# Where the second expert's list is written and where the registers are loaded, in a fused attention and mixture-of-experts block

## The chip, the cores and the metric

The kernel runs on one core of a Trainium2 chip. The metric is the device time of one execution in microseconds. Before the change three runs took 1684.58, 1686.65 and 1686.75 us, so the median is 1686.65 us. The execution that the hardware profiler recorded took 1661.85 us, and the span from its first to its last instruction is 1660.0 us.

## The reference

One transformer block on x of shape (2, 2048, 256), float32. A conditioning vector gives shifts, scales and gates (`sa, ca, ga, sb, cb, gb`); the gates are kept at least 0.25 away from zero.

```python
h = _layernorm(x, axis=-1) * (1 + ca) + sa
x = x + ga * _L0_attn_ref(h, ...)        # 2 query heads of 128, one key and value head, rope, causal
h = _layernorm(x, axis=-1) * (1 + cb) + sb
x = x + gb * _L0_ffn_ref(h, ...)
```

The second part is a mixture of eight experts with a threshold of its own for each token:

```python
gate = jax.nn.softmax(x @ Wg + bg, axis=-1)
thr = jax.nn.sigmoid(x @ Wt + bt) * MAX_THRESHOLD
adapted = gate - thr
mask = (adapted >= 0).astype(x.dtype)
w = adapted * mask          # then divided by its sum over the experts
h = jax.nn.gelu(jnp.einsum('td,edf->etf', x, W1) + b1[:, None, :])
eo = jnp.einsum('etf,efd->etd', h, W2) + b2[:, None, :]
out = jnp.einsum('te,etd->td', w, eo)
```

With the inputs used, 2640, 2609, 2370, 2710, 2418, 2886, 3614 and 1806 of the 4096 tokens have a weight above zero for experts 0 to 7. The kernel computes an expert only for the tokens on its list.

## The kernel before

**Two phases.** `attention` works through 32 tiles of 128 tokens, the two batches in turn in groups of 4, 4, 4, 2, 1 and 1 tiles. `experts` then works through items of 256 tokens of one expert, expert after expert. Line numbers here are those of the kernel before, which the profile names too.

**Attention and its planner.** Every step of this phase (a few instructions on one engine) is handed to `Plan.add` with an engine, an assumed cost, what it follows, what it takes of a fixed number of buffers and gives back, a rank, and a time `late` after which its result is there. `Plan.run` then plays the steps through once, always giving an idle engine the ready step of the lowest rank, and emits the instructions in the order found. So one more step, or another cost or rank, can move every later step on all engines. A tile's steps are layer norm (statistics on VectorE, the power to -1/2 on GpSimd, L425 and L426), projections, rope, scores (L541), exponentials on ScalarE (L568), their transposes (L614), the product with the values (`pav`, L624), the output projection (`po`, L658), the residual, the second layer norm (`hx`), a copy of it as high and low halves (L690) which goes to the DRAM tensor `feats`, and the logits (`pl`). For each group `gate_steps` computes weights (`entry`), counts tokens on TensorE (`pc`, L797 and L800) and from that each token's place on the list of every expert (`place`, up to L818). An indirect DMA from GpSimd's queue for each tile then writes the entries of expert 0 to its list in DRAM (`scatter`, L821). Each of these waits for the one before it on the list.

**Work ahead.** When 24 tiles are listed, the head of list 0 is read (L919) and two items of expert 0 (AHEAD = 2, 512 tokens) are worked on within attention: `fetch` gathers their rows from `feats` (GpSimd, L897), transposes them by a DMA of SyncE's queue (L906) and joins the halves (VectorE, L912); then come matmuls `pha` (L963), Gelu (L971), matmuls `pya` (L980), and `result` (L987, L990). These steps have rank 1000, behind everything else. Their first matmuls and their Gelu follow the last tile's exponentials, which need another table on ScalarE. In the same way the whole list 0 is read (L1018) and the item after these two is fetched to xT (`_next`). `total` (L865 to L884) writes the count of every list to `counts`, less the 512 tokens worked on ahead (for expert 0, 2128 remain), and, for each list, two numbers that steer how the next one is written: how many items it has that are followed by another one (at most NP = 8), and 8 less that.

**The expert phase.** It opens with a barrier of all engines. Each engine has a program of its own with loops, and waits on semaphores. `count` (L1051) loads a number of `counts` into a register of an engine; TensorE and ScalarE load eight, VectorE nine, before their first work. An item is fetched in a chain: GpSimd copies two indices for each partition (`at`, L1312) and gathers the rows to `xr` (L1270, two indirect DMAs); SyncE transposes xr to `xp` (L1116); VectorE joins the halves into `xT` (`ready`, L1212) when TensorE has finished the item's first matmuls. There is one xr, one xp and one xT. TensorE runs eight pairs of matmul groups, `h` (L1158) and `y` (L1149), with Gelu on ScalarE between them (L1184). VectorE adds the bias (`yb`, L1236), names the rows (`who`, L1240), clears the second half of `yo` where an item has only 128 tokens (L1247) and multiplies with the gates (`yo`, L1248). GpSimd adds yo to the rows of the output by indirect DMAs (L1301). VectorE names rows and writes yo only when the scatter before the last has landed. ScalarE issues the weights of expert e + 2, 2 MB, when it reaches expert e (L1193, L1196).

**How lists 1 to 7 are written.** A list has 32 tiles of entries, in 8 parts of 4 tiles. GpSimd writes a part of list e + 1 (`write`: two copies, L1283 and L1286, and four scatters, L1291) within the fetch of an item of expert e, between that item's gathers and the scatter of a result. As many parts as are not carried so are written ahead of the expert's items. Ahead of everything, `write(1, 0, 0)` writes part 0 of list 1 once more, so that every later part has one before it to wait for. SyncE reads list e + 1 (L1106) when all its parts have landed, and GpSimd begins the items of expert e + 1 only after that.

## Time and profile before

| what | value |
| --- | --- |
| median of three runs | 1686.65 us |
| profiled execution | 1661.85 us |
| its span | 1660.0 us |
| TensorE busy | 1613.9 us, 97% of the span |
| VectorE, ScalarE busy | 659.0 us (40%), 584.4 us (35%) |
| GpSimd busy | 904.5 us (54%) |
| mean granted TensorE clock | 0.992 of full speed |
| last matmul ahead ends, first expert matmul starts | 482.2 us, 490.42 us |
| last matmul ends | 1647.5 us |

PE is TensorE's matmuls, PEld its weight loads, DVE VectorE, ACT ScalarE, POOL GpSimd and SP SyncE; a q behind a name is the engine's sequencer or its DMA queue. A row of the timeline has start and length in microseconds, engine, line, operation, output and inputs, the number of instructions, and in brackets how long the engine was idle before it and what ended that. The chain of waits is followed back from the last instruction: at each step to what released it. In the table by stretches, each engine's busy time in a stretch stands in the order PE, PEld, DVE, ACT, POOL, and behind it the granted clock as a share of full speed, the share of the 16 DMA engines, and GB/s.

### The profile page before, as it was taken

The page shows a single profiled execution, that of the slowest core. Times are in us where ns is not written, and L with a number is a line of the kernel's source. Part 1 is how long each engine was busy: PE and PEld are TensorE (multiplying, and loading weights), DVE is VectorE, ACT ScalarE, POOL GpSimd, SP SyncE. Part 2 cuts the span into 40 slices and gives each one's busy share as a digit, 9 for nine tenths or more (in the row PEclk, how much of TensorE's full clock was granted, in tenths as well). Part 3 has the DMA queues.
Part 4 walks back from the last instruction along what each step waited for, and adds up shares of the span by engine and source line. Part 5 has one row for each costly group of instructions (what it writes and reads, how often), then busy time and mean ns, then how long its engine had stood idle before and what let it go on. Part 6 is the DMA issues. An engine that isn't in the chain of part 4 may idle for free.

```text
span 1660.0 us, 26742 instructions
## 1 busy us (share of the span) xinstructions
PE 1613.9 (97%) x7666; PEld 1347.2 (81%) x7666; DVE 659.0 (40%) x2148; ACT 584.4 (35%) x1416; POOL 904.5 (54%) x1037
## 2 busy tenths in 40 slices
PE   8999999999989979999999999999999999999996
PEld 5667677777768868888888888888888888888886
DVE  7987656656532322223222222222322232222322
ACT  3555555555522222222222222222222222222222
POOL 5563522211237767756776774676677477644443
PEclk9999999999989999999999999999999999999999
DMA  5411000000133353335335333533533333333432
GB/s 182 150 39 34 26 30 29 14 14 13 33 84 60 60 106 57 60 62 111 57 64 112 59 59 66 102 61 62 112 60 59 59 58 60 66 57 57 66 57 46
DMA packets 166045, 106.36 MB, mean 64 GB/s; under 512 B 111136, under 2 KB 157344, under 8 KB 165856
## 3 DMA queue, kind: packets, MB, share of 16 engines
q0 software_dynamic: 42064, 46.84, 17.8%
q1 hardware_dynamic: 116048, 46.22, 11.8%
q10 hardware_dynamic: 7872, 12.58, 2.4%
q8 instruction: 26, 0.43, 0.1%
q14 instruction: 35, 0.29, 0.1%
HBM read 50.39 MB, written 31.87 MB: 50 GB/s over the span
## 4 chain that ended last, share of the span: by engine, by line
PE 61%; DMA 3%; POOL 3%; issue 3%; POOLq 1%; DVE 0%; DVEq 0%; SPq 0%
PE h L1158 31%; PE y L1149 31%; DMA xp<-xr 2%; POOL out L1301 2%; DMA xr<-feats,at 1%; POOL list L1291 1%; POOL xr L1270 0%; DMA out<-yo,who 0%; DMA sign_p_next<-g_sb_r_next 0%; DMA g_sb_r_next<-feats,next_at 0%; POOLq L1051 0%; POOL out L1333 0%; POOL at L1312 0%; POOLq L1099 0%; POOLq L1312 0%
## 5 line engine op out<-in xcount | busy, mean ns | idle before, releaser
L1158 PE MATMUL h<-xT,w 128*128 128x256 f32 (+1 forms) x2752 | 659.2, 372 | 19.9 <-DVE xT L1212 11.6
L1149 PE MATMUL y<-w,g 128*128 128x256 f32 x2640 | 654.1, 379 | 0.0
L1184 ACT ACTIVATE g<-h,b_sb 128x256 f32<-128x256 f32 (+1 forms) x688 | 320.5, 466 | 849.9 <-PE h L1158 848.3
L1158 PEld LDWEIGHTS h<-xT,w 128*128 128x128 f32 x2752 | 514.0, 191 | 90.1 <-DVE xT L1212 13.3
L1149 PEld LDWEIGHTS y<-w,g 128*128 128x128 f32 x2640 | 498.5, 190 | 66.1
L1301 POOL DMA_INDIRECT out<-yo,who x173 | 282.5, 1633 | 212.7 <-DVE yo L1248 161.2
L1212 DVE COPY xT<-xp 128x512 uint16<-128x512 uint16 x172 | 67.9, 437 | 628.2 <-PE h L1158 602.8
L1291 POOL DMA_INDIRECT list<-new,to x228 | 232.8, 1021 | 99.3 <-POOL new L1286 46.7
L1270 POOL DMA_INDIRECT xr<-feats,at x172 | 174.3, 1013 | 100.9 <-POOL at L1312 70.2
L541 PE MATMUL psc<-kT,qT 128*128 128x512 f32 (+3 forms) x320 | 143.7, 534 | 0.0
L624 PE MATMUL pav<-pT,v 128*128 128x256 f32 x544 | 142.9, 385 | 0.0
L552 DVE TENSOR_SCALAR_CACHE_REDUCE s<-psc 128x512 f32<-128x512 f32 (+3 forms) x160 | 96.0, 604 | 67.4 <-PE psc L541 48.9
L568 ACT ACTIVATE s<-s,nmx 128x512 f32<-128x512 f32 (+3 forms) x160 | 103.8, 650 | 47.0 <-DVE nmx L559 46.8
L624 PEld LDWEIGHTS pav<-pT,v 128*128 128x128 f32 x544 | 95.9, 190 | 28.8 <-issue 20.9
L1236 DVE TENSOR_TENSOR yb<-y,b_bc 128x256 f32<-128x256 f32 x165 | 62.7, 420 | 136.1 <-PE y L1149 136.1
L618 ACT COPY pT<-ptr 128x512 f32<-128x512 f32 (+1 forms) x144 | 76.8, 564 | 47.9 <-PE pav L624 32.5
L1227 DVE SCALAR_TENSOR_TENSOR gate<-gb_bc,mcur,part 128x256 f32<-128x256 f32 x172 | 75.8, 482 | 3.0
L425 POOL TENSOR_SCALAR rstdf<-mvf 128x1 f32<-128x1 f32 x32 | 8.2, 257 | 122.7 <-DVE mvf L421 70.7
L614 PE MATMUL ptr<-ident,s 128*128 128x128 f32 x544 | 72.6, 274 | 2.1 <-ACT s L568 1.9
L614 PEld LDWEIGHTS ptr<-ident,s 128*128 128x128 f32 x544 | 63.1, 141 | 13.1 <-ACT s L568 4.9
L1312 POOL COPY at<-sheet 128x2 int32 x85 | 62.9, 740 | 14.5 <-DMA xp<-xr 13.5
L821 POOL DMA_INDIRECT list<-entry,place x32 | 33.5, 1048 | 62.4 <-DVE place L818 26.8
(159 smaller groups left out, 1098.6 us busy)
## 6 DMA issues: line engine op xcount, KB each, us to landing
w<-in_w ACTq DMA_DIRECT2D x12, 1024.0 KB, 7.8
x<-in_x SPq DMA_DIRECT2D x32, 128.0 KB, 2.1
out<-x SPq DMA_DIRECT2D x32, 128.0 KB, 1.7
feats<-hp SPq DMA_DIRECT2D x32, 128.0 KB, 1.7
w<-in_w SPq DMA_DIRECT2D x4, 1024.0 KB, 9.1
list<-new,to POOLq DMA_INDIRECT x228
out<-yo,who POOLq DMA_INDIRECT x173, 3.9
xr<-feats,at POOLq DMA_INDIRECT x172
```

What stands on the lines that cost most here:

```text
L541: nc.tensor.matmul(ps[:, :w], st["qT"][:, h, :], kT[:, ds(c * SC, w)], start=True, stop=not last)
L552: nc.vector.tensor_scalar(s[:, :w], st["sc", h, c][:, :w], 1.0, None, ALU.mult, ALU.max, accum_out=st["mx", h][:, c : c + 1],)
L568: nc.scalar.activation(s[:, :w], s[:, :w], AF.Exp, bias=st["nmx", h], accum_out=st["den"][:, h, c : c + 1],)
L614: nc.tensor.transpose(ptr[:, j, h, :], s[:, ds((c0 + j) * P % SC, P)], ident)
L618: nc.scalar.copy(pT[:, :m], st["ptr", c0][:, :m])
L624: nc.tensor.matmul(st["pav"][:, : NH * P], v[:, c0 + j, :], st["pT", c0][:, j].rearrange("p h t -> p (h t)"), start=(c0 + j == 0), stop=(c ...
L1149: last = pe.matmul(ys[c], gs[f % 4][:, ts(c, P)], weights[e][1][:, f, :], start=(f == 0), stop=(f == NF - 1),)
L1158: last = pe.matmul(hs[f % 4][:, :w], weights[e][0][:, k, ts(f, P)], xT[:, k, :w], start=(k == 0), stop=(k == KD - 1),)
L1184: act.activation(gs[f % 4][:, :w], hs[f % 4][:, :w], AF.Gelu_apprx_tanh, bias=b1_sb[:, at : at + 1],).then_inc(sem["act"], 1)
L1270: pool.indirect_dma_start(out=xr[:, ts(c, 2 * D)], out_offset=None, in_=feats, in_offset=bass.IndirectOffsetOnAxis(ap=at[:, c : c + 1], ax ...
L1291: pool.indirect_dma_start(out=lists[e], out_offset=bass.IndirectOffsetOnAxis(ap=to[:, j : j + 1], axis=0), in_=new[:, j, :], in_offset=Non ...
L1301: pool.indirect_dma_start(out=rows, out_offset=bass.IndirectOffsetOnAxis(ap=who[:, c : c + 1], axis=0), in_=yo[:, c, :], in_offset=None, b ...
```

## The change

1. **Two parts of list 1 in attention.** The first FRONT = 2 parts of list 1, tiles 0 to 7 in the order of tokens (the first eight of batch 0), are scattered in attention, each tile by one indirect DMA from `entry` and `place`, as list 0 is, with a rank 10 higher. In the expert phase expert 0's items carry at most 6 parts (2 to 7), the numbers in `counts` are capped to suit, and `write(1, 0, 0)` becomes one scatter of tile 0.
2. **Items ahead.** Their first matmuls follow the last tile's last `pav` step (`last_sum`) in place of its exponentials; their Gelu still follows the exponentials. The read of the head of list 0 no longer follows the last scores.
3. **The next item first.** The fetch of the item behind those two has rank 999.
4. **Registers in the plan.** Steps `hold` at the end of the plan load the registers before the barrier: eight each on TensorE (behind its last matmul ahead) and ScalarE, nine on VectorE, four on GpSimd, two on SyncE. `count` then takes the register, and loads only what was not held.
5. **The last half item.** If the last item of expert 7 has 128 tokens, its rows and its result go to `who_end` and `yo_end`; VectorE neither waits for the scatter before nor clears a half.

```diff
+FRONT = 2
@@ attention, tile_steps and gate_steps
+        last_sum[:] = n_p[-1:]
-        def scatter(j):
+        def scatter(e, j):
             nc.gpsimd.indirect_dma_start(
-                out=lists[0],
-                out_offset=bass.IndirectOffsetOnAxis(ap=place[:, at + j, 0:1], axis=0),
-                in_=entry[:, at + j, 0, :],
+                out=lists[e],
+                out_offset=bass.IndirectOffsetOnAxis(ap=place[:, at + j, e : e + 1], axis=0),
+                in_=entry[:, at + j, e, :],
...
         for j in range(m):
-            listed.append(plan.add(
-                "POOL", 1.1, lambda j=j: scatter(j), after=[n] + listed[-1:], rank=r + 10.0,
-                late=1.5,
-            ))
+            for e in (0, 1):
+                if e == 0 or at + j < FRONT * NW:
+                    listed[e].append(plan.add(
+                        "POOL", 1.1, lambda e=e, j=j: scatter(e, j), after=[n] + listed[e][-1:],
+                        rank=r + 10.0 * (e + 1), late=1.5,
+                    ))
@@ total
+        nc.vector.tensor_scalar(n[:, :1], n[:, :1], float(NP - FRONT), None, ALU.min)
         nc.vector.tensor_copy(counts[:, E : 2 * E], n)
         nc.vector.tensor_scalar(
-            counts[:, 2 * E : 3 * E], n, -1.0, float(NP), ALU.mult, ALU.add
+            counts[:, 2 * E : 2 * E + 1], n[:, :1], -1.0, float(NP - FRONT), ALU.mult, ALU.add
+        )
+        nc.vector.tensor_scalar(
+            counts[:, 2 * E + 1 : 3 * E], n[:, 1:], -1.0, float(NP), ALU.mult, ALU.add
         )
@@ items ahead, the next item, registers
-    n_front = low("SP", 0.1, read_front, listed_ahead + last_score, late=2.5)
+    n_front = low("SP", 0.1, read_front, listed_ahead, late=2.5)
-                "PE", 1.74, lambda f0=f0, first=first: first(f0), [n_x, l_first[0]] + before_gelu,
+                "PE", 1.74, lambda f0=f0, first=first: first(f0),
+                [n_x, l_first[0]] + last_sum,
...
+    def next_(eng, cost, do, after=(), **how):
+        return plan.add(eng, cost, do, after=after, rank=999.0, **how)
+    n_behind = next_("DVE", 0.4, behind, [n_s, n_flag])
+    fetch(lambda c: next_at[:, c : c + 1], "_next", [n_behind], lambda: kept.xT, low=next_)
...
+    def hold(name, eng, columns):
+        def load():
+            kept.count[name] = {at: register(nc, eng, counts, at) for at in columns}
+        return load
+    low("PE", 2.0, hold("PE", nc.tensor, range(E)), [n_total] + n_ahead)
+    low("ACT", 2.0, hold("ACT", nc.scalar, range(E)), [n_total] + n_a)
+    low("DVE", 2.2, hold("DVE", nc.vector, [*range(E), skip]), [n_total, n_behind])
+    low("POOL", 1.0, hold("POOL", nc.gpsimd, [skip, 0, E, 2 * E]), [n_total])
+    low("SP", 0.5, hold("SP", nc.sync, [0, E]), [n_total, n_s])
@@ experts, SyncE's read of a list
-                    sync.wait_ge(sem["written"], (e * NP + 1) * (16 * NW))
+                    sync.wait_ge(sem["written"], (e * NP - FRONT) * (16 * NW) + 16)
@@ experts, VectorE's item
-                    dve.wait_ge(sem["added"], t * (16 * CI) + 2 * (16 * CI))
+                    end = e == E - 1 and parts < CI
+                    if not end:
+                        dve.wait_ge(sem["added"], t * (16 * CI) + 2 * (16 * CI))
                     dve.tensor_copy(
-                        who, mcur[:, :, 2:3].bitcast(I32).rearrange("p c o -> p (c o)")
+                        who_end if end else who,
+                        mcur[:, :, 2:3].bitcast(I32).rearrange("p c o -> p (c o)"),
                     ).then_inc(sem["named"], 1)
...
-                    if parts < CI:
+                    if parts < CI and not end:
                         dve.memset(yo[:, parts:, :], 0.0)
                     dve.tensor_tensor(
-                        yo[:, :parts], yb[:, :parts], gate[:, :parts], ALU.mult
+                        (yo_end if end else yo)[:, :parts], yb[:, :parts], gate[:, :parts],
+                        ALU.mult,
                     ).then_inc(sem["biased"], 1)
@@ experts, GpSimd
-                write(1, 0, 0)
+                pool.indirect_dma_start(
+                    out=lists[1],
+                    out_offset=bass.IndirectOffsetOnAxis(ap=place[:, 0, 1:2], axis=0),
+                    in_=entry[:, 0, 1, :],
+                    in_offset=None,
+                ).then_inc(sem["written"], 16)
...
                 with pool.If(single > 0):
-                    add(t0 + 1, 1)
+                    add(t0 + 1, yo_end, who_end, 1)
```

More of the change, by code (lines that the diff above doesn't have):

```diff
@@ L160, in adaln_block_kernel @@
         xT=const.tile([P, KD, TI], F32, name="xT"),
+        count={},
     )
@@ L186, in adaln_block_kernel @@
     at = ep.tile([P, CI], I32, name="at")
+    yo_end = ep.tile([P, 1, D], F32, name="yo_end")
+    who_end = ep.tile([P, CI], I32, name="who_end")
     mcur = ep.tile([P, CI, ENT], F32, name="mcur")
@@ L193, in adaln_block_kernel @@
         tc, nc, lists, feats, out.rearrange("b t d -> (b t) d"), counts, ident, b1_sb, b2_bc,
-        gb_bc, w1, w2, weights, xr, xp, kept, gs, gate, part, yb, sheets, at, mcur, to, new,
+        gb_bc, w1, w2, weights, xr, xp, kept, gs, gate, part, yb, yo_end, who_end, sheets, at, mcur, to, new,
         place, entry, hs, ys,
@@ L836, in gate_steps @@
         for j in range(m):
-            listed.append(plan.add(
-                "POOL", 1.1, lambda j=j: scatter(j), after=[n] + listed[-1:], rank=r + 10.0,
-                late=1.5,
-            ))
+            for e in (0, 1):
[4 more added lines that the diff above has]
+                    ))
         return n
-    order_w, listed, last_exp = [], [], []
+    order_w, listed, last_exp, last_sum = [], ([], []), [], []
     groups = [(0, 4), (1, 4)] * 3 + [(0, 2), (1, 2), (0, 1), (1, 1), (0, 1), (1, 1)]
@@ L853, in attention @@
         if q == AHEAD_TILES:
-            listed_ahead = list(listed)
+            listed_ahead = list(listed[0])
             def filled(group=group):
@@ L888, in low, with fetch @@
         return plan.add(eng, cost, do, after=after, rank=1000.0, **how)
-    def fetch(index, u, after, to, take=()):
+    def fetch(index, u, after, to, take=(), low=low):
         st = {}
@@ L1015, in attention @@
         low("DVE", 1.5, result, [n, n_g, l_b2], give=["ps", "size"])
+        n_ahead = [n]
     n_s = low(
-        "SP", 0.1, lambda: nc.sync.dma_start(kept.sheet, sheet_of_0), listed, late=2.0
+        "SP", 0.1, lambda: nc.sync.dma_start(kept.sheet, sheet_of_0), listed[0], late=2.0
     )
@@ L1030, in behind, with register @@
         )
-    n = low("DVE", 0.4, behind, [n_s, n_flag])
-    fetch(lambda c: next_at[:, c : c + 1], "_next", [n], lambda: kept.xT)
-    plan.add("PE", 0.2, total, after=[last, n_flag], take=["ps"], give=["ps"], rank=q)
+    def next_(eng, cost, do, after=(), **how):
+        return plan.add(eng, cost, do, after=after, rank=999.0, **how)
+    n_behind = next_("DVE", 0.4, behind, [n_s, n_flag])
+    fetch(lambda c: next_at[:, c : c + 1], "_next", [n_behind], lambda: kept.xT, low=next_)
+    n_total = plan.add(
+        "PE", 0.2, total, after=[last, n_flag], take=["ps"], give=["ps"], rank=q, late=2.0
+    )
+    def hold(name, eng, columns):
+        def load():
+            kept.count[name] = {at: register(nc, eng, counts, at) for at in columns}
+        return load
+    skip = 3 * E
+    low("PE", 2.0, hold("PE", nc.tensor, range(E)), [n_total] + n_ahead)
[3 more added lines that the diff above has]
+    low("SP", 0.5, hold("SP", nc.sync, [0, E]), [n_total, n_s])
     plan.run()
     ctx.close()
+def register(nc, eng, counts, at):
+    return nc.values_load(
+        counts[0:1, at : at + 1], engines=[eng.engine],
+        skip_runtime_bounds_check_because="from a sum of 0s and 1s over all tokens",
+        min_val=0, max_val=NTOK if at < E else NP if at < 3 * E else AHEAD * CI,
+    )
 def experts(
     tc, nc, lists, feats, rows, counts, ident, b1_sb, b2_bc, gb_bc, w1, w2, weights, xr, xp, kept,
-    gs, gate, part, yb, sheets, at, mcur, to, new, place, entry, hs, ys,
+    gs, gate, part, yb, yo_end, who_end, sheets, at, mcur, to, new, place, entry, hs, ys,
 ):
@@ L1048, in experts, with count @@
     xT, who, yo = kept.xT, kept.who, kept.yo[-1]
-    def count(eng, at, most):
-        return nc.values_load(
-            counts[0:1, at : at + 1], engines=[eng.engine],
-            skip_runtime_bounds_check_because="from a sum of 0s and 1s over all tokens",
-            min_val=0, max_val=most,
-        )
+    eng_name = {
+        nc.tensor.engine: "PE", nc.scalar.engine: "ACT", nc.vector.engine: "DVE",
+        nc.gpsimd.engine: "POOL", nc.sync.engine: "SP",
+    }
+    def count(eng, at):
+        held = kept.count[eng_name[eng.engine]]
+        return held[at] if at in held else register(nc, eng, counts, at)
     def run(eng, many, most, do):
@@ L1120, in _ @@
                 for e in range(E):
-                    many = items_of(sync, count(sync, e, NTOK))
+                    many = items_of(sync, count(sync, e))
                     if e == E - 1:
@@ L1124, in _ @@
                     else:
-                        a = count(sync, E + e, NP)
+                        a = count(sync, E + e)
                         run(sync, a, NP, lambda i: turn(t0 + done + i))
@@ L1172, in _ @@
                 pe.sem_inc(sem["taken"], 1)
-                n = [count(pe, e, NTOK) for e in range(E)]
+                n = [count(pe, e) for e in range(E)]
                 items(pe, n, item, begin)
@@ L1200, in _ @@
                 act.sem_inc(sem["second"], 4)
-                items(act, [count(act, e, NTOK) for e in range(E)], item, begin)
+                items(act, [count(act, e) for e in range(E)], item, begin)
             @block.vector
@@ L1254, in begin @@
                         dve.wait_ge(sem["read"], 16 * e)
-                n = [count(dve, e, NTOK) for e in range(E)]
-                skip = count(dve, 3 * E, AHEAD * CI)
+                n = [count(dve, e) for e in range(E)]
+                skip = count(dve, 3 * E)
                 dve.sem_inc(sem["ready"], 2)
@@ L1275, in gather, with write @@
                         ).then_inc(sem["loaded"], 16)
-                def write(e, c, w=None):
-                    if w is None:
-                        w = c + (e - 1) * NP
-                        wait("written", w * (16 * NW) + 16 * NW)
-                        w = w + 1
+                def write(e, d):
+                    first = FRONT if e == 1 else 0
+                    w = d + ((e - 1) * NP - FRONT if e > 1 else 0)
+                    c = nc.s_assert_within(
+                        d + first, first, NP - 1,
+                        skip_runtime_bounds_check_because="a part of a list",
+                    )
+                    wait("written", w * (16 * NW) + 16)
                     pool.tensor_copy(
@@ L1296, in write, with scatter @@
                         ).then_inc(sem["written"], 16)
-                def scatter(parts=CI):
+                def scatter(yo, who, parts):
                     for c in range(parts):
@@ L1316, in fetch, with add @@
                     gather(t)
-                def add(t, parts=CI):
+                def add(t, yo=yo, who=who, parts=CI):
                     wait("added", t * (16 * CI))
                     wait("biased", t + 1)
-                    scatter(parts)
+                    scatter(yo, who, parts)
                 def item(e, i, t, also=None):
@@ L1343, in _ @@
                 pool.sem_inc(sem["biased"], AHEAD)
-                write(1, 0, 0)
-                skip = count(pool, 3 * E, AHEAD * CI)
+                pool.indirect_dma_start(
[4 more added lines that the diff above has]
+                ).then_inc(sem["written"], 16)
+                skip = count(pool, 3 * E)
                 done, t0 = 1, 0
                 for e in range(E):
-                    many = items_of(pool, count(pool, e, NTOK))
+                    many = items_of(pool, count(pool, e))
                     if e > 0:
@@ L1353, in _, with part @@
                     else:
-                        a, front = count(pool, E + e, NP), count(pool, 2 * E + e, NP)
-                        def part(c):
-                            write(e + 1, nc.s_assert_within(c, 0, NP - 1,
-                                skip_runtime_bounds_check_because="a part of a list"))
-                        run(pool, front, NP, part)
+                        a, front = count(pool, E + e), count(pool, 2 * E + e)
+                        most = NP - FRONT if e == 0 else NP
+                        def part(d):
+                            d = nc.s_assert_within(d, 0, most - 1,
+                                skip_runtime_bounds_check_because="a part of a list")
+                            write(e + 1, d)
+                        run(pool, front, most, part)
                         run(pool, a, NP, lambda i: item(
@@ L1381, in _ @@
                 single = pool.snap(
-                    ((count(pool, E - 1, NTOK) + (P - 1)) >> 7) & 1, min_val=0, max_val=1
+                    ((count(pool, E - 1) + (P - 1)) >> 7) & 1, min_val=0, max_val=1
                 )
                 with pool.If(single > 0):
-                    add(t0 + 1, 1)
+                    add(t0 + 1, yo_end, who_end, 1)
                 with pool.If(single < 1):
```

## The prediction

> **What bounds the kernel now.** I read the waits of TensorE first, from 440 us (the last attention tile) to the end. Columns: who waited, for whom, us in total, times, longest.

> ```profile
> PE h L1158 <- DVE xT L1212: 11.6, 1, 11.6
> PE h L1158 <- DVEq L1051: 8.2, 1, 8.2
> ```

> TensorE is otherwise busy without a gap, so only these two stops, the work before 440 us and the tail after the last matmul can give anything. Then the chain that ended last, around the larger stop (start, length, what):

> ```profile
> 579.01 2.74 DMA xr<-feats,at
> 581.98 3.05 DMA xp<-xr
> ...
> 607.07 2.76 DMA xr<-feats,at
> 610.05 11.37 DMA xp<-xr
> 622.26 4.24 PE h L1158 x12
> ```

> Before 622 us the chain runs on GpSimd, item after item; after it, on TensorE alone. The fetch at 607 us is the first of expert 1. It could not start earlier: SyncE reads list 1 (L1106, issued at 601.08) only when GpSimd has written the eighth part of it, whose last scatter (L1291) began at 598.96 in the last but one fetch of expert 0. So its gather landed at 609.8 and its transpose started at 610.05, half a microsecond after ScalarE had issued the 2 MB of weights of expert 3 (L1193, L1196, 609.40 and 609.82): 11.37 us instead of 3.05. What the stop costs is read from VectorE's copies of xT, here and at the end of expert 2, which also closes with a half item:

> ```profile
> 601.17 0.87 DVE L1212 COPY xT<-xp 128x512 uint16<-128x512 uint16 x2 [5.99 <-PE h L1158]
> 621.44 0.76 DVE L1212 COPY xT<-xp 128x512 uint16<-128x512 uint16 x2 [12.71 <-DMA xp<-xr]
> 635.28 0.76 DVE L1212 COPY xT<-xp 128x512 uint16<-128x512 uint16 x2 [10.21 <-PE h L1158]
> ```

> ```profile
> 890.99 0.77 DVE L1212 COPY xT<-xp 128x512 uint16<-128x512 uint16 x2 [8.02 <-PE h L1158]
> 899.32 0.76 DVE L1212 COPY xT<-xp 128x512 uint16<-128x512 uint16 x2 [2.43 <-PE h L1158]
> 911.91 0.97 DVE L1212 COPY xT<-xp 128x512 uint16<-128x512 uint16 x2 [6.29 <-PE h L1158]
> ```

> The same three copies are 34.11 us apart in the one and 20.92 in the other: the stop costs **13.2 us**, 11.6 of waiting and the rest matmuls at the lower clock after it.

> The smaller stop is the handoff. TensorE's last matmul ahead ends at 482.2, VectorE's xT copy (L912) at 485.35, and then every engine loads its counts (L1051); columns: count, ns min/median/max, first and last start.

> ```profile
> L1051 DVEq TENSOR_LOAD <-counts x9: 301/310/595, 486.2 to 489.1; - x9
> L1051 PEldq TENSOR_LOAD <-counts x8: 294/306/562, 486.5 to 489.2; - x8
> ```

> The first expert matmul starts at 490.42. Last, the tail, from the same chain view:

> ```profile
> 1644.97 3.88 DMA out<-yo,who
> 1648.85 0.02 issue
> 1648.87 0.18 DVE who L1240
> ```

> VectorE had the last half item's biased sum (yb) at 1647.93, and waited for a landing before it could name its rows.

> **The change part by part**, in the profiled execution's time (1661.85 us for a span of 1660.0, so 1.85 around it).

> *Two parts of list 1 move out of the expert phase.* A fetch of expert 0 takes GpSimd 13.43 us with a part (its index copies L1312 go from 509.08 to 589.67 in six steps), TensorE 13.81 us an item. A part is two copies and four scatters, from 513.01 to 519.02, 6.0 us, and about 6.3 with the gap behind. Of nine items t=0 to 8 the fetches t=1 to 8 now carry a part each; the change caps the number at 6, so t=1 to 6 carry parts 2 to 7 and t=7 and 8 none. GpSimd's doubled first part (489.94 to 496.58) also shrinks to one scatter of 1.0 us, and its four loads are gone from there. Its first index copy thus comes 4 to 5 us earlier, near 492. The sixth part is written by 492+5x13.43+9.3 = 568.5, has landed at 570.7 (scatter to landing 2.2 us), and list 1 is read about 30 us before the fetch of its first item can use it. With two fetches of 7 us instead of 13.4 GpSimd is then held by a free xp, not by its own work. TensorE starts the half item at 487.8 (below)+16.35+7x13.81 = 600.8 and expert 1 7.1 later. Expert 1's first transpose starts when the half item's copy has emptied xp, near 599.4, and takes 3.05 us, since the weights come only at about 606.6; it is needed at about 606. The transpose behind it meets the weights: 607.5+11.4 = 618.9, needed at 619.2, and VectorE's copy still ends a microsecond before TensorE asks. The end of expert 3 shows that this passes: a transpose issued at 1050.97, 0.6 us after the weights, and no stop. So **-13.2**. Bounds: -13.2 to -3.4, if the first transpose collides too (8.3 us longer) and its own lead of some 3.5 us hides none of it, with the 1.5 us of low clock.

> *The eight scatters in attention* (L821 doubled for tiles 0 to 7) lie on GpSimd between 95 and 200 us, where it is busy 49.5 of 105 us and TensorE idles 3 us in all. By the rows of the 14 list scatters there:

> ```profile
> L821 POOL DMA_INDIRECT list<-entry,place x14 | 14.9, 1067 | 22.3 <-DMA list<-entry,place 10.3 <-DVE place L818 9.0 <-DVE rd L601 1.4
> L525 PE MATMUL pr<-ident,t 128*128 128x128 f32 x27 | 4.5, 275 | 1.5 <-POOL t L518 1.5
> L464 PE MATMUL pt<-ident,xn 128*128 128x128 f32 x20 | 3.7, 276 | 1.3 <-POOL xn L455 1.3
> ```

> 8 x 1.07 = 8.5 us on GpSimd, plus waits of 0.3 to 3.3 us for the scatter before on the same list; the two lists alternate, so part of those waits is now filled. Behind them on GpSimd stand the reciprocal roots (L425, L426) and the halves, for which VectorE and then TensorE wait. [...] The row says otherwise: 957 to 1259 ns from the quickest to the slowest with VectorE busy 26 of 35 us. I go by the row. The planner, though, orders everything behind the first new scatter anew on all engines, with the same matmuls. TensorE loses 3 us between 95 and 200 us now and 2 us after it, so an order can give back 4 us at most; lose, more. I take **0**, from -3 to +6.

> *Items ahead behind the last tile's sums, fetch of the next item ranked first.* The first ahead matmuls wait for the last tile's pav, no longer for its exponentials: they move past two pav steps, no work is removed. The last tile's projection, logits and places come about 1.75 us earlier (one group of 8 matmuls). The second item's y now directly follows the first item's y in the same PSUM place, so TensorE waits for VectorE's sum (0.76 us, L987) and its register loads in front of it: about **+1.15**; before, a group of h matmuls covered the sum.

> *Register loads in the plan.* VectorE's nine (3.1 us) lie before the first result and beside TensorE; ScalarE's, SyncE's and GpSimd's lie in idle time, and GpSimd's 1.4 us delay only the gather of the next item, which has 4 us of slack before VectorE is free at 484. TensorE's eight take 3.0 us behind its last matmul, which are not hidden by matmuls but run beside VectorE's result and xT copy (0.76+0.69+0.16+0.76 us). Step by step: the last matmul ends at 483.3, both engines are done near 485.7 to 486.0; from there the barrier took 1.15 us to TensorE's first instruction (485.35 to 486.5) and the branch 0.9 to the first matmul: 487.8 instead of 490.42. That is **-2.6**, with the 1.15 above in it; bounds 0 and -5. Nothing was won by it before, since GpSimd set the pace of expert 0; with the stop gone TensorE sets it from here to the end.

> The clock in this gap is the second place to weigh a rule (PEclk is the column behind the busy times):

> ```profile
> 482.20:484.00 1.80, 0.00 (x0) 0.00 (x0) 1.52 (x4) 0.00 (x0) 0.00 (x0) 1.00 0.75 144
> 484.00:486.00 2.00, 0.00 (x0) 0.00 (x0) 0.76 (x2) 0.00 (x0) 0.00 (x0) 0.79 0.01 2
> 486.00:488.00 2.00, 0.00 (x0) 0.00 (x0) 0.00 (x0) 0.00 (x0) 1.03 (x1) 0.50 0.01 4
> ```

> The clock halved some 3 us into the gap and the first item took 16.35 us (490.42 to 506.77) instead of 13.81: 2.5 lost. [...] By the row it is lost again; I take the row and keep 2.5 for the range.

> *The last half item's own place.* Its rows are named straight after yb, and the memset goes: yo ended at 1649.80, now 1647.93+0.04+0.17+0.2+0.36 = 1648.7. GpSimd is free from 1646.5, so the last scatter starts **1.1** us earlier. Cover gone: none, it is the end of the chain.

> Sum: -13.2+0-2.6-1.1 = -16.9, so 1644.95 for the profiled execution. The median of the runs shown is 24.8 us (1.5%) above it, and no row says where they lie. Stretched evenly, the gain is 17.1; if TensorE alone were slower, GpSimd would be less behind and the gain near 15. I take 16.9 off the median: **1669.8 us**.

> **Rivals.** (a) *Clock stays up or the new order helps*: -2.5 or so more, 1664 to 1667. [...] (b) *The stop is only halved, or attention gives some back*: the collision moves with the weights, which ScalarE now issues 2.5 us earlier too, beside the transpose of item 1. +4 to +10: 1674 to 1680. Against it: the end of expert 3. (c) *Slower*: in-order GpSimd. A list scatter that waits for the one before it (up to 3.3 us) stands ahead of a reciprocal root; eight times 1.07+3.3 is 35 us, and if half of it reaches TensorE, whose reserve of other tiles is what covers it now, all is lost: 1687 to 1692. It decides from 17 us of new idle before 440 us. Against it: all present GpSimd waits of TensorE there come to 3.5 us. (d) *Nothing moves*: the read of list 1 still waits for the last fetch. Against it: parts are capped at 6 and the count of list 0 gives 8.

> **How the numbers follow.** As worked 0.56 (its own range 1667 to 1673), (a) 0.15, (b) 0.19, (c) 0.07, (d) 0.03. Range 1661 to 1680 leaves out (c), (d) and the ends of (a) and (b). Within 0.2% (3.4 us, about what a measurement of this kernel tells from no change) 0.04, from (d) and the edge of (c); slower 0.06; faster 0.90.

> **What would show it.** No wait of h for xT at the first change of expert; three copies 21 us apart there; the first expert matmul 4 to 5 us behind the last one ahead, and no loads between; list scatters 40 in attention and 217 behind; the last scatter within 1 us of its product. It is wrong if TensorE shows new waits on GpSimd between 95 and 200 us, or if the transposes of expert 1 last 11 us with TensorE idle behind them.

## The result, and the profile after

In the first comparison the changed kernel took 1671.38 us (median of 8 runs, 1668.0 to 1679.12) and the kernel before, beside it, 1686.51 (8 runs). The ratio is 0.992, with a 95% interval of 0.9897 to 0.9943. Against the 1686.65 us of the prediction that is 15.3 us less; 16.9 had been forecast. Two later comparisons on other chips gave 1644.01 against 1659.68 (0.9904, interval 0.9889 to 0.992) and 1660.29 against 1677.99 (0.9905, interval 0.9882 to 0.9928).

First TensorE's waits from 440 us to the end, in the first profiled execution of the changed kernel (1669.28 us, span 1667.5):

```profile
PE y L1193 <- ACT g L1228: 10.4, 8, 2.4
PE h L1202 <- DVEq L1306: 4.7, 1, 4.7
PE y L1193 <- issue: 4.6, 5, 2.1
PE ptr L618 <- ACT s L572: 1.9, 1, 1.9
```

The wait of h for xT, 11.6 us before, is gone. The handoff (second row) fell from 8.2 to 4.7 us. The first and third rows, 15 us together, are new beside the profile of before, and nothing in the change accounts for them: most of them lie where a half item or a new expert begins. A second profiled execution, on another chip (1644.55 us, span 1642.7), has none of them. The same view of it, complete:

```profile
PE h L1202 <- DVEq L1306: 4.7, 1, 4.7
PE ptr L618 <- ACT s L572: 1.9, 1, 1.9
```

So the steps of the sum are read from this second execution where those waits would hide them. VectorE's three copies at the first change of expert there:

```profile
597.72 0.78 DVE L1256 COPY xT<-xp 128x512 uint16<-128x512 uint16 x2 [8.03 <-PE h L1202]
606.03 0.79 DVE L1256 COPY xT<-xp 128x512 uint16<-128x512 uint16 x2 [2.35 <-PE h L1202]
618.68 1.00 DVE L1256 COPY xT<-xp 128x512 uint16<-128x512 uint16 x2 [4.78 <-DMA xp<-xr]
```

They are 20.96 us apart, from 34.11. The second copy now waits for TensorE, not for its transpose. The third still waits for its transpose, yet TensorE does not idle behind it. Why this transpose came late is seen in four rows of the same execution: ScalarE's two issues of weights, the second half of the gather by GpSimd, and the transpose.

```profile
605.95 0.38 ACTq L1237 DMA_DIRECT2D w<-in_w  x1
606.36 0.50 ACTq L1240 DMA_DIRECT2D w<-in_w  x1
609.20 0.98 POOL L1318 DMA_INDIRECT xr<-feats,at  x1 [0.30 <-issue]
615.43 1.24 SPq L1160 DMA_TRANSPOSE xp<-xr  x1
```

Here it is the gather that lies beside the 2 MB of weights: SyncE waited for it until 615.43, 6.2 us behind the issue of its second half, where the fetch shown in the prediction needed 3.0 (607.07 to 610.05). The transpose itself then took 3.2 us (to VectorE's copy at 618.68), beside 3.05 for the one at 581.98 in the prediction.

The handoff in the first profile: TensorE's last group ahead and first expert group, then the loads of registers by sequencer (count, ns min/median/max, first and last start).

```profile
474.93 8.80 PE L992 MATMUL pya<-w,s_g 128*128 128x256 f32 x40
488.39 5.31 PE L1202 MATMUL h<-xT,w 128*128 128x256 f32 x12 [4.67 <-DVEq L1306]
```

```profile
L1076 DVEq TENSOR_LOAD <-counts x9: 302/308/550, 474.4 to 477.7; - x9
L1076 PEldq TENSOR_LOAD <-counts x8: 300/308/811, 479.7 to 483.2; - x8
```

The last matmul ahead ends at 483.72. All loads lie in front of that, TensorE's own too. VectorE's last copy to xT (485.23, 0.76 long) ends at 485.99, and 2.40 us later the first expert matmul starts, at the half clock (0.50): twelve matmuls take 5.31 us, and twelve of the same size at 600.52, at 1.00, take 2.75.

Last the end of the first profile, from the chain of waits and from the timeline:

```profile
1653.09 3.84 DMA out<-yo,who
...
1657.19 0.03 POOLq L1352
```

```profile
1656.25 0.42 DVE L1295 TENSOR_TENSOR yo_end<-yb,gate 128x256 f32<-128x256 f32 x1
1657.95 1.55 POOL L1352 DMA_INDIRECT out<-yo_end,who_end  x1 [3.29 <-issue]
```

VectorE no longer waits for the landing of the scatter before, but GpSimd does: the product was done at 1656.67, the landing came at 1656.93, and the scatter began at 1657.95.

### The profile page after: what moved, and what is told of

Its sections match the earlier page's. It is cut to its first block, busy times and chain, and to the rows that moved or that the text cites. A ratio compares the mean times of both kernels' runs of the same rounds, so it can differ in the third digit from the quotient of the medians.

```text
span 1667.5 us, 26732 instructions
## 1 busy us (share of the span) xinstructions
PE 1621.9 (97%) x7666; PEld 1349.4 (81%) x7666; DVE 660.7 (40%) x2144; ACT 582.1 (35%) x1417; POOL 912.0 (55%) x1032
## 3 DMA queue, kind: packets, MB, share of 16 engines
q1 hardware_dynamic: 116048, 46.22, 12.1%
## 4 chain that ended last, share of the span: by engine, by line
PE 67%; issue 1%; DMA 1%; another core or an unknown queue 1%; POOL 1%; POOLq 0%; DVE 0%; ACT 0%; SPq 0%; DVEq 0%; ACTq 0%
PE y L1193 33%; PE h L1202 33%; DMA list<-entry,place 0%; POOL out L1352 0%; DMA out<-yo,who 0%; ACT g L1228 0%; DMA xp<-xr 0%; DMA xr<-feats,at 0%; POOL list L1342 0%; POOL out L1385 0%; POOLq L1143 0%; DVE xT L1256 0%; DVE yb L1280 0%; DVE yo L1295 0%
## 5 line engine op out<-in xcount | busy, mean ns | idle before, releaser
L1193 PE MATMUL y<-w,g 128*128 128x256 f32 x2640 | 658.2, 381 | 15.3 <-ACT g L1228 10.4
L1193 PEld LDWEIGHTS y<-w,g 128*128 128x128 f32 x2640 | 498.6, 190 | 86.0 <-ACT g L1228 11.9
L1352 POOL DMA_INDIRECT out<-yo,who x172 | 282.2, 1641 | 231.2 <-DVE yo L1295 178.2
L1342 POOL DMA_INDIRECT list<-new,to x216 | 227.7, 1054 | 93.6 <-issue 75.3
L826 POOL DMA_INDIRECT list<-entry,place x40 | 42.6, 1066 | 74.2 <-DVE place L823 43.4
L1363 POOL COPY at<-sheet 128x2 int32 x85 | 61.2, 720 | 10.5 <-DMA xp<-xr 10.5
```

The source lines that it names most:

```text
L1193: last = pe.matmul(ys[c], gs[f % 4][:, ts(c, P)], weights[e][1][:, f, :], start=(f == 0), stop=(f == NF - 1),)
L1342: pool.indirect_dma_start(out=lists[e], out_offset=bass.IndirectOffsetOnAxis(ap=to[:, j : j + 1], axis=0), in_=new[:, j, :], in_offset=Non ...
L1352: pool.indirect_dma_start(out=rows, out_offset=bass.IndirectOffsetOnAxis(ap=who[:, c : c + 1], axis=0), in_=yo[:, c, :], in_offset=None, b ...
```

## The experiments

The main theory is the prediction's: the two parts written early take the stop at the first change of expert away, and the loads and the last half item are small gains on TensorE's path. The rivals: one part would do, or attention gives something back; the loads are hidden anyway; the half clock eats what a shorter gap gives. This is what the profiled executions show of TensorE at the handoff. "Rest" is the span less the start of the first expert matmul. The four rows from before_again on come from one chip, the four from after_timed on from another, the last two from a third.

| kernel | last matmul ahead ends | idle | first expert matmul | rest |
| --- | --- | --- | --- | --- |
| before (first profile) | 482.19 | 8.23 | 490.42 | 1169.6 |
| changed (first profile) | 483.72 | 4.67 | 488.39 | 1179.1 |
| before_again | 484.05 | 8.24 | 492.29 | 1168.7 |
| after_again | 482.39 | 4.69 | 487.08 | 1155.6 |
| front0 | 483.82 | 4.39 | 488.21 | 1168.0 |
| parts_alone | 483.64 | 7.31 | 490.95 | 1156.6 |
| after_timed | 485.13 | 4.70 | 489.83 | 1155.8 |
| noreg | 482.57 | 7.32 | 489.89 | 1155.9 |
| front4 | 482.34 | 4.40 | 486.74 | 1155.3 |
| split | 484.62 | 3.33 | 487.95 | 1156.3 |
| after_third | 482.11 | 4.69 | 486.80 | 1170.8 |
| front1 | 488.41 | 4.70 | 493.11 | 1171.0 |

**The waits at half items: both kernels, profiled a second time.** No edit.

> The kernel before, unchanged, profiled once more. The first profiled execution of it took 1661.85 us, all its other runs 1681 to 1693. Theory A[...]: in most executions the engines stop where a loop is left and a half item or the next expert begins[...]; the first profile of before happened to show none of it. Then this profile lies near 1680 to 1690, shows y of TensorE waiting for g of ScalarE for 10 to 20 us in pieces of 0.5 to 2.5 us at the changes of expert, as the changed kernel's profile does (10.4 us in 8 pieces), and the stop at 610 us is as before. Theory B (the change brought these waits, since its loops and loads lie elsewhere in the code): this profile shows none of them again, and the 25 us lie somewhere else, for example in longer fetches of GpSimd.

> The changed kernel, unchanged, profiled once more. Both theories: 1668 to 1679 us; no wait of h for xT at the change from expert 0 to 1; y waiting for g some 8 to 20 us in all. If the waits at the changes of expert are a matter of the execution, their places and lengths differ from the first profile's; if they belong to the code, they are the same to 0.2 us.

Measured: 1662.78 and 1644.55 us, one run each; the kernel before had a median of 1660.23 there (19 runs). The expected times of both runs, those of the first chip, were missed. Neither kernel shows one wait of y for g after the handoff, and TensorE has 0.1 us of idle between 500 us and the tail in the changed one. So the new order of work alone does not bring these waits. Two further comparisons, of the change itself:

> The change itself, timed beside the kernel before on one chip. If its first time (1671 against 1686) and the look on the second chip (1644.6 against 1660) are the same gain on two chips, the ratio here is 0.990 to 0.993 again (1643 to 1647 us where the kernel before takes 1660). If the waits of ScalarE and TensorE at the entry of half items, which the first profile of it showed and the second did not, belong to the new order of work, the ratio goes above 0.995.

> The change itself beside the three kernels of this call, so that they are compared with it on one chip: 1643 to 1647 us again, with a gap of 4.4 to 4.7 us and the half clock for 6.8 us from about 2.6 us into it.

Measured: 1644.01 us (0.9904) and 1660.29 us (0.9905). On the chip of after_third the changed kernel shows the waits again:

```profile
PE y L1193 <- ACT g L1228: 9.5, 10, 1.9
PE h L1202 <- DVEq L1306: 4.7, 1, 4.7
PE ptr L618 <- ACT s L572: 1.9, 1, 1.9
PE y L1193 <- issue: 1.0, 2, 0.6
```

There it takes 16.3 us more than on the chip of after_timed, and the kernel before takes 18.3 us more. The ratio is the same with and without them, so they go with the chip or its state, not with the change. That the kernel before has the very same waits where it takes 1678 or 1686 us is not shown, as no profile of it comes from such runs. The expected 1643 to 1647 us for the last run was a time of the other chips, and missed.

**Part 1 taken out.**

```diff
-FRONT = 2
+FRONT = 0
```

> The changed kernel with FRONT = 0: no part of list 1 in attention, all eight parts in the fetches of expert 0, everything else as changed. My theory (the stop between expert 0 and 1 is what the change takes away, 13.2 us): the stop is back, h waits for xT once for 8 to 12 us at about 608 to 620 us, less by some of GpSimd's 5 us earlier start; 8 to 13 us slower than the changed kernel, 1679 to 1685, and at most 4 to 6 us faster than before. Rival (the stop goes because GpSimd's first part is one scatter and not five, and its registers are loaded early, so that it starts 5 us sooner): no stop, within 3 us of the changed kernel.

Measured: 1658.05 us, ratio 0.9981 (0.9973 to 0.9989), 13.5 more than the one run of the change on this chip. The stop is back, and the handoff stays short:

```profile
PE h L1202 <- DVE xT L1256: 9.2, 1, 9.2
PE h L1202 <- DVEq L1306: 4.4, 1, 4.4
```

**Part 1 alone**, on the kernel before: the scatters of two parts in attention, the caps in `counts`, the new arguments of `write` and the wait before the read, nothing of the items ahead, the loads and the last half item.

```diff
+FRONT = 2
...
-        def scatter(j):
+        def scatter(e, j):
...
+            for e in (0, 1):
+                if e == 0 or at + j < FRONT * NW:
...
-                    sync.wait_ge(sem["written"], (e * NP + 1) * (16 * NW))
+                    sync.wait_ge(sem["written"], (e * NP - FRONT) * (16 * NW) + 16)
```

> The kernel before with the parts of list 1 moved and nothing else (FRONT = 2, the caps, the one scatter in place of the doubled part): registers, items ahead and the end are as before. My theory: 12 to 14 us faster than before (13.2, and TensorE's handoff, end and attention as before), 1672 to 1675, and 2 to 4 us slower than the changed kernel. Rival (the registers give most): within 4 us of before.

Measured: 1648.59 us, ratio 0.9923 (0.9909 to 0.9936). No stop, and the handoff still idles 7.3 us. The rest of the span is 1156.6 us, against 1168.7 for the kernel before: 12.1 of it is the stop. With that, 11.6 us come from part 1 and 2.2 from all else, by medians; both together gave 15.7 on that chip, by the one run of the change. The 1.9 us between the sum of the halves and the whole lie inside the intervals, so it stays open whether the handoff is worth less while the stop stands.

**One part early, and four.**

```diff
-FRONT = 2
+FRONT = 1          # front1
+FRONT = 4          # front4
```

> The change with one part of list 1 written in attention instead of two; the fetches 1 to 7 of expert 0 carry a part each and only the last carries none. Theory (what counts is that list 1 is read before the last fetch of expert 0 ends): the list is read near 587 us, its first gather lands near 600 and its transpose is needed near 606, so there is no wait of h for xT at the first change of expert and the time is within 1.5 us of the change. Rival (the two free fetches were both needed): h waits 4 to 8 us for xT there, and the kernel takes 4 to 8 us more than the change.

> Four parts of list 1 written in attention instead of two: 16 scatters between 95 and 200 us where the change has 8 (no work left out). By the row of the list scatters (1.04 us each, GpSimd busy 56 of 105 us) there is still room: 0 to 2 us slower than the change, since two parts already took the stop away. Rival, [...] GpSimd's own order (a scatter that waits for the one before on its list stands ahead of a reciprocal root): scatters well above 1.3 us or new waits of TensorE for GpSimd there, and 8 us or more lost.

Measured for four: 1644.37 us beside 1644.01, that is nothing. The eight more scatters lie behind 200 us, not before it as the expectation had them (tiles 8 to 15). They are as quick as the others (ns min/median/max), and TensorE waits 2.1 us for GpSimd in all of attention, beside 1.9 in the change:

```profile
L826 POOL DMA_INDIRECT list<-entry,place x48: 955/1013/1364, 96.3 to 468.8; - x48
```

Measured for one: 1666.32 us beside 1660.29, so 6.0 more (ratios 0.9934 and 0.9905; the intervals, 0.9914 to 0.9953 and 0.9882 to 0.9928, overlap a little). Yet the stop is gone as the theory had it: no wait of h for xT, and the rest of the span is 1171.0 beside 1170.8 us. The whole loss lies in front of the first expert matmul, which comes 6.3 us later in the profile. Of that, 2.6 us are there by 153 us, before the two programs differ at all; five profiles, four of the change and this one, spread as far at that matmul (153.2 to 156.2 us). The other 3.7 come behind it, and there it is the planner: the change has the first of the four scatters at 161 us, and without them the same 2274 matmuls ahead of the first expert matmul stand in another order from the 741st on. TensorE idles 2.3 us more there than in the change, and behind two waits close together, 0.65 and 1.55 us, its clock is 0.50. TensorE's timeline, then the table by stretches (busy PE, PEld, DVE, ACT, POOL, granted clock, DMA share, GB/s):

```profile
256.24 0.41 PE L468 MATMUL pt<-ident,xn 128*128 128x128 f32 x2 [0.65 <-DVE ge L791]
258.93 1.02 PE L719 MATMUL pl<-wgt_sb,hT 128*128 128x9 f32 x4 [1.55 <-DVE col L816]
```

```profile
255.36:258.77 3.41, 1.29 (x8) 0.62 (x6) 3.17 (x14) 3.19 (x11) 3.01 (x4) 1.00 0.12 41
258.77:262.19 3.42, 3.26 (x11) 2.80 (x12) 2.00 (x11) 0.63 (x2) 2.32 (x3) 0.50 0.01 1
262.19:265.60 3.41, 3.41 (x15) 3.14 (x14) 0.41 (x1) 1.76 (x3) 1.78 (x2) 0.50 0.01 1
```

6.7 us of work at half clock lose 3.3; the change lost 1.7 in the same way behind 440 us (after_third: granted 0.96 from 440 to 480 us; front1: 1.00), so the clock costs 1.6 more. With the 2.3 of idle that is 3.9 for the 3.7 seen. The rival's size (4 to 8 us) was met, but not by its mechanism.

**The loads taken out of the plan.**

```diff
-            kept.count[name] = {at: register(nc, eng, counts, at) for at in columns}
+            kept.count[name] = {}
```

> The change without the register loads in the plan: the steps that hold counts load nothing, so every engine loads its counts behind the handoff as before. Theory (TensorE sets the pace from the handoff to the end, and the loads are on its path): the gap of 4.7 us before the first expert matmul becomes 7.3 to 8.2, and 2 to 3.5 us are lost against the change, 1647 to 1648 where the change takes 1644.6. Rival (GpSimd still sets the pace of expert 0): the gap grows but the time stays within 1 us of the change.

Measured: 1647.62 us, ratio 0.9934 (0.992 to 0.9948), beside 1644.01 for the change: 3.6 more. The idle time is 7.32 us instead of 4.70, and 5.66 us of the work behind it ran at the half clock instead of 4.95, which loses 0.4 more; 3.0 together. (The one profile of the change on this chip is its slowest run, 1647.46 us: its attention ended late, so the table shows the gap and not the gain.) TensorE sets the pace from the handoff on, and the loads were on its path. As all engines load late here at once, whose loads count is not separated.

**Half the result ahead of the last matmul.** The sums of the two halves of an item ahead get a PSUM place each and a result step each, and the next item's xT copy stands ahead of the last result.

```diff
-        low("DVE", 1.5, result, [n, n_g, l_b2], give=["ps", "size"])
...
+            low(
+                "DVE", 0.8, lambda c=c, result=result: result(c), [n, n_g, l_b2],
+                give=["ps", "size"] if c == CI - 1 else ["ps"],
+            )
...
-    fetch(lambda c: next_at[:, c : c + 1], "_next", [n_behind], lambda: kept.xT, low=next_)
+    fetch(lambda c: next_at[:, c : c + 1], "_next", [n_behind], lambda: kept.xT, low=next_, late=0.5)
```

> The change, with the y of the two halves of an item ahead in a PSUM place each and a result step for each half; the next item's xT copy on VectorE stands ahead of the last result. No work is left out. What VectorE does behind TensorE's last matmul ahead shrinks from 2.3 us (sum, product, copy) to about 0.9. Theory: the gap goes from 4.7 to about 3.3 us, so 1.4 us are won against the change; if the granted clock then stays up over the gap, 2.5 more (first item in 13.8 instead of 16.3 us). Rival (the barrier alone sets the gap, or the copy waits for its gather): the gap stays above 4.3 us and the time within 1 us of the change.

Measured: 1643.98 us beside 1644.01. The idle time is 3.33 us, as the theory had it, and the time is the rival's. In the rows the clock gives one reason. The stretches by intervals of the clock, in split and then in after_again (the first row of each is the one ahead of the drop):

```profile
483.66:487.07 3.41, 0.96 (x5) 0.51 (x3) 1.61 (x4) 0.00 (x0) 0.00 (x0) 1.00 0.01 2
487.07:490.48 3.41, 2.53 (x6) 2.08 (x7) 1.68 (x5) 0.42 (x1) 2.35 (x2) 0.50 0.65 207
490.48:493.90 3.42, 3.42 (x9) 2.70 (x9) 0.00 (x0) 0.95 (x3) 2.27 (x4) 0.50 1.02 332
```

```profile
481.58:484.99 3.41, 0.80 (x4) 0.38 (x2) 2.19 (x6) 0.00 (x0) 0.00 (x0) 1.00 0.00 0
484.99:488.40 3.41, 1.32 (x3) 1.15 (x4) 1.38 (x5) 0.00 (x0) 1.47 (x1) 0.50 0.35 66
488.40:491.82 3.42, 3.42 (x9) 2.70 (x9) 0.29 (x1) 0.95 (x2) 2.81 (x4) 0.50 0.99 373
```

The half clock lasts 6.83 us in both, counted from the drop. The shorter gap only moves more work into it: 5.95 us instead of 4.74, so 0.6 of the 1.4 us go back. The 0.8 left over is less than these runs can tell, and where it went is open.

**The clock held up by added matmuls.**

```diff
+    def warm():
+        pw = ps_tile("pw")
+        for f in range(12):          # 6 in warm_split, which is made from split
+            nc.tensor.matmul(
+                pw[:, :D], weights[0][0][:, f % KD, ts(f % 2, P)], weights[0][1][:, f % KD, :],
+                start=True, stop=True,
+            )
+
+    n_warm = low("PE", 2.64, warm, n_ahead, take=["ps"], give=["ps"])
...
```

> The change with twelve matmuls of 128x256 on weights behind the last matmul ahead, 2.6 us on TensorE, whose sums nobody reads (work added, none left out). They lie under VectorE's 2.3 us of sum, product and copy, so TensorE idles only about 2.1 us before the first expert matmul. Theory ([...] the runs so far show it dropping at up to 28% busy): with 2.1 us of idle at least 38% of any such interval is busy, the clock stays at 1.00, and 2.4 us are won against the change (1641.6 where it takes 1644.0). Rival (2 us of idle suffice): the clock halves all the same and the time is that of the change or up to 0.5 us above.

> Both: the result of each half ahead in its own place, as tried before, and six such matmuls (1.3 us) behind the last matmul ahead. The gap in real work is 3.3 us, or up to 0.5 more if the added matmuls hold up the barrier; TensorE idles 2.0 to 2.4 us. Theory: the clock stays up, so that the shorter gap (1.4 us) and the clock (2.4 to 3.0 us) both count: 3 to 4 us faster than the change, 1640 to 1641 where it takes 1644. Rival (the clock halves): within 1 us of the change, as for the split alone, since what the shorter gap gives the half clock takes.

Measured: 1663.49 us (0.9914) and 1665.15 us (0.9924), beside 1660.29 for the change (0.9905); intervals overlap, and nothing is won. A matmul written here is two in the trace (an item ahead's sixteen of pya are 32), so the twelve took 5.3 us, not 2.6, and held up the barrier. In warm the real gap became 7.6 us: 2.9 more for the 2.4 of clock won, so the test of the clock was paid for with what it was to win. The clock itself: in warm TensorE idled 2.41 us and stayed at 1.00 throughout. In warm_split it idled 2.38 us and the clock halved all the same:

```profile
486.00:488.00 2.00, 0.04 (x1) 0.05 (x1) 0.17 (x1) 0.00 (x0) 0.20 (x1) 1.00 0.02 4
488.00:489.40 1.40, 1.40 (x7) 1.25 (x8) 1.33 (x5) 0.28 (x1) 1.40 (x1) 1.00 0.97 187
489.40:492.80 3.40, 3.40 (x10) 2.69 (x9) 0.17 (x1) 1.14 (x3) 2.79 (x4) 0.50 1.01 374
```

The expected 38% is what 2.1 us of idle leave of 3.41 us, the shortest stretch of half clock in these profiles. The theory that this is enough fell: in the 3.41 us ahead of this drop TensorE was busy 1.44, or 42%. The waits at half items add to the noise of this chip (13.5 us of them in the profile of warm_split, 10.5 in that of the change), so a difference of 1 us could not be read there. No version tried beats the change beyond its uncertainty.

## Why the prediction was right

*The stop.* Right in place and size. Forecast -13.2. The rest of the span fell from 1169.6 (first profile of before) to 1155.6 us: 14.0, of which 0.8 is the tail, so 13.2. The pair on one chip gives 13.1 less 0.8, 12.3, as the stop itself was 9.7 us there instead of 11.6. Part 1 alone gave 12.1 in the profile and 11.6 by medians. The first transpose of expert 1 met no weights, as forecast. The second item came late and was covered, and its copy began at 618.68, beside 618.9 forecast for the end of its transpose. That agreement is luck: the sum had the transpose meet the weights and last 11.4 us, but the gather met them and was late by 3 us, and the transpose took 3.2. A slip in the reading did no harm: the eighth part was written in the last fetch of expert 0 (the one at 591 us, for the half item), not in the last but one.

*The eight scatters.* Right, by the row: with 20 instead of 14 list scatters between 95 and 200 us their mean is 1044 ns in the first profile and 1040 in the second, from 1067. But the value 0 was luck inside the right bounds: front1, with four scatters fewer, took 6.0 us more, and its profile puts 3.7 of them on the planner's new order, a mechanism the prediction named (everything behind the first new scatter is ordered anew). Rival (b) could have come that way.

*The handoff.* Mechanism right; of the sum, two terms were not there. TensorE did not wait 1.15 us for VectorE's sum between the two items: in the second profile the sum came at 476.72 while the 40 matmuls of both items run without a gap to 482.39. And TensorE's loads do not follow its last matmul. Its sequencer took them while matmuls queued before were still at work (479.7 to 483.2, last matmul to 483.72). So the 2.27 us of VectorE's sum, product and copy set the pace; behind the last matmul, the loads of 3.0 us would have been the longer of the two. From VectorE's copy to the first expert matmul it took 2.40 us, not 2.05. The errors nearly cancel: the gap was 4.67 for a forecast of 4.5. The first expert matmul came 2.03 us earlier in the first pair, 5.2 in the second (forecast 2.6), but the end of the last matmul ahead alone lies between 482.1 and 485.1 in four profiles of the very same kernel. That term can't be judged closer than this; the gap can, and it shrank by 3.6 us.

*The clock.* The row was right: in all twelve profiles of the table, with gaps of 3.33 to 8.24 us, the clock fell to 0.50, 2.23 us (after_third) to 3.29 us (front0) behind the last matmul. That it could stay up over a gap of 4.5 us was the author's estimate, and rival (a) did not happen.

*The tail.* The step "GpSimd is free from 1646.5, so the last scatter starts 1.1 us earlier" is the term that was mis-sized: it measured 0.8. `add` on GpSimd itself waits for every scatter before it to have landed, so the wait that was taken from VectorE was met again on GpSimd, 0.3 us after the product was done (1656.67, landing 1656.93), and the scatter came another 1.0 us later. From yb to the last scatter it takes 2.3 us (2.32, 2.31, 2.28 in three kernels with the part) instead of 3.1 to 3.2 (3.16, 3.08 without): 0.8. The scatter began 1.3 us after its product, not within 1 us.

*The 24.8 us* between profile and median of the kernel before: no row said where they lie. In the changed kernel the first profile falls 23.4 us behind the second after the handoff, matmul for matmul, and does so at the new waits (15 us) and in the matmuls around them, some at the half clock. That the 24.8 us of the kernel before lie in the same places is likely and not shown. Where those waits are absent, the forecast for the profiled execution, 1644.95, met 1644.55.

## What to carry to other kernels

When an in-order engine writes a list that the next stage must read, count back from the read to the last write, and move a few early writes to where that engine has idle time; the transfer behind the read then starts ahead of the heavy loads it would have met (in the second profile it was issued at 598.59 us and the weights at 605.95; in the kernel before it started at 610.05, behind them, and took 11.37 us; what comes behind it may meet them, and needs slack). A wait taken off one engine is worth only what the next engine's own wait leaves (0.8 of the 1.1 us forecast here), so read the code of both before sizing it. Where a planner orders the work, the cost of a small edit is more than that of its own instructions: measure the neighbouring values (here 0, 1, 2 and 4) before believing that one of them is free.

## What the runs showed of the hardware

**The half clock lasted 3.41, 6.83 or 10.24 us.** Read from TensorE's granted clock, which is 0.50 in these stretches and 1.00 around them:

| kernel | idle | half clock from, to | length | busy in the 3.41 us before |
| --- | --- | --- | --- | --- |
| before | 8.23 | 485.15, 495.39 | 10.24 | 13% |
| noreg | 7.32 | 485.31, 495.55 | 10.24 | 20% |
| after_again | 4.69 | 484.99, 491.82 | 6.83 | 23% |
| split | 3.33 | 487.07, 493.90 | 6.83 | 28% |
| warm_split | 2.38 | 489.40, 492.82 | 3.41 | 42% |
| front1, in attention | 0.65 and 1.55 | 258.77, 265.60 | 6.83 | 38% |
| warm | 2.41 | none | | |

This also tells warm from warm_split. Cut at the steps of its own clock (a drop near 1654.2 us), the gap of warm falls across two intervals, which were 62% and 67% busy; that of warm_split falls into one, 42% busy. The gaps are equal, 2.41 and 2.38 us, so between these two runs it was luck.

At the handoff the clock came back behind an interval that was busy throughout (before, 491.98 to 495.39 us; 3.41 us or more of 3.41 in noreg, after_again and split). Elsewhere it came back behind one that was 83% busy (before, at 625.10 us), while it stayed at 0.50 behind 74% (split, 487.07 to 490.48) and once even behind 95% (front1, 258.77 to 262.19). In these profiles a gap cost its length plus about half of the work done at 0.50 behind it (in before twelve matmuls took 5.29 us there, from 490.42, and 2.75 at 1.00, from 506.77), and a shorter gap had more of that work: 4.74 us in after_again, 5.95 in split.

**TensorE's register loads ran beneath its own matmuls.** In the first profile of the changed kernel they took 0.30 us each (one 0.81), from 479.7 to 483.2 us, and TensorE was busy 4.03 of the 4.30 us from 479.7 to 484.0.

**Waits where half items and experts begin**, on two of four chips or states of a chip. For example, at the first change of expert in the first profile:

```profile
606.69 0.69 PE L1193 MATMUL y<-w,g 128*128 128x256 f32 x2 [2.08 <-issue]
608.82 0.70 PE L1193 MATMUL y<-w,g 128*128 128x256 f32 x2 [0.99 <-ACT g L1228]
```

They are 10 to 15 us in all, and behind two of them, of 2.40 and 2.41 us, the clock fell to 0.50 (in the first profile at 892.75 and 1182.88 us). Most lie where engines go on to a piece of their program that they have not just run; a few do not (0.67 us at 574.5, 1.17 at 1211.9). No run took such a piece away, so the cause is open.
